# A graph layer with segment maximum: a reordered head, and a fifth matmul tile in every eighth chunk

## The chip, the core and the metric

The kernel runs on one core of one Trainium2 chip. The metric is the device time of one execution in microseconds (us). Engines are named as in the profile: PE (matmul) with its weight loads PEld, DVE (VectorE), ACT (ScalarE), POOL (GpSimd) and SP (SyncE, which here only issues DMAs). SPq, ACTq and POOLq are the queues in which DMAs are issued.

## The reference

There are 12,500 nodes with 32 features and 400,000 edges, sorted by their target node `dst`; `src` is random.

```python
h = jnp.maximum(_layernorm(x, axis=-1), 0.0)
e_feat = jnp.concatenate([h[src], h[dst], edge_attr_32], axis=-1)   # 400000 x 96
v = jax.nn.relu(e_feat @ W1 + b1) @ W2 + b2                         # 96 -> 64 -> 32
x_cand = jax.ops.segment_max(v, dst, num_segments=num_nodes)
x = x + jnp.maximum(x_cand, h)
```

## The kernel before

**Tiling.** The edges are cut into four stripes of 100,352 and these into 196 chunks of 512. A chunk is worked on for all four stripes at once, so 128 partitions hold 4 stripes x 32 features. The loop (`for c in range(0, NCH, 2)`) finishes two chunks, c and c + 1, in a step and makes ready a = c + 2 and b = c + 3. There are 98 steps.

**The three parts of the first layer** are summed in PSUM tiles `ph`, in this order: the edge features `ea` (`edges_into`, L527); the target nodes (`windows_into`, L527): the product h @ W1[32:64] is made once for all nodes and kept in DRAM as `q_d`, and since targets are sorted a chunk of one stripe needs 32 rows of it, loaded by SP as `qw` (8 loads in a step, L480), with a one-hot `of` that ACT makes from the targets `db` (`window_hots`, L486 and L487); and the source nodes `ht` (L527), which close the sum.

**Source rows.** A chunk needs 16 tiles of 128 rows of h.
- 12 are gathered by POOL, one indirect DMA each (L159), three in one buffer `gh` of 18, and transposed by DVE into `ht` (L274).
- 4 come by matmuls (`tile`, L256 to L261): the node number is split into 128 x 7 keys and 14 places. h stands in SBUF as `hs`, a sum of two rounded parts in 7 groups. For a tile, 7 x 2 matmuls 128x448 multiply one-hots `hot` with `hs` into a PSUM tile `pv`; DVE multiplies by the mask of the place (`one`, L260) and reduces over the 14 places into `gm` (L261). The one-hots are made from keys `kb` loaded from DRAM: groups 0 to 4 by DVE (L225), 5 and 6 by ACT (L234 and L235).
- The first two chunks use none of this: their rows of x are gathered ahead (`raw_gather`, 8 gathers a time into `xg`) and normalized in place (`raw_1`, `raw_2`, `raw_3`).

**Then**: ACT's relu `hid` (L574), the second layer on PE (L586), a running segment maximum as a scan of DVE over the edges (L594), with penalties `pb` that are -1e30 where a new target begins, transposes and a selection of the last edge of each target on PE (L500, L511), and writes into `top_d`, which was filled with zeros before (L547). Penalties are made in the head from `de`, the targets in another layout (L449, L450), written to DRAM (`pen_d`, L451) and loaded as `pb` for four chunks at a time, as are `ea` and `db` (`load`, L465 to L469).

**Order of work.** The order on SP, PE, DVE and ACT is that of the code, written out by hand. POOL's instructions are nearly all gathers. In a step PE does: `ph<-ht`; transposes L500; `tile(a, 1)`; `edges_into(a)`; L586; `windows_into(a)`; L511; then seven tiles without a break (a 2, a 3, b 0 to b 3, and tile 0 of the next chunk), 98 matmuls. The buffers of the head (pool `nodes`) and of the loop (pool `edges`) lie in the same memory, so the first load of the loop waits for the head's last use. Every fourteenth chunk DVE does `make_block`, seven small operations.

**The head** on SP: loads of x; `h_d` writes; `key_d`, `kb`, `de`; seven `q_d` writes; `pen_d`; then `ea`, `db`, `pb` of chunks 0 to 3 and 32 `qw` loads of chunks 0 to 3.

Of the kernel before, what the change touches and what calls it, by code (L numbers as in the profile page):

```python
# [12 lines left out]
I32 = mybir.dt.int32  # L13
# [32 lines left out]
MM = 4  # L46
MMC = range(2, NCH - 1)
SOME = 3
AHEAD = 4
# [18 lines left out]
def gnn_kernel(ctx, tc, x, src, src_mm, src_t, dst, dst_ext, lo, lo_c, ends_b, edge_attr, weights, w1, w2, b2, out):  # L68
# [21 lines left out]
    dram = ctx.enter_context(tc.tile_pool(name="dram", bufs=1, space=DRAM))  # L90
    gathered = ctx.enter_context(tc.tile_pool(name="gathered", bufs=18))

# [3 lines left out]
    top_d = [dram.tile([NP, D], F32, name=f"top_d{k}") for k in range(2)]  # L96
    key_d = dram.tile([len(MMC) * MM * P], F16, name="key_d")
    acc_d = dram.tile([NP, D], F32, name="acc_d")
# [32 lines left out]
    hs = const.tile([P, 2, A1, D, A0], F32R, name="hs")  # L131
    place_k = const.tile([P, len(MMC) * MM], F32, name="place_k")

# [19 lines left out]
    def gather(c):  # L153
        n = min(K - MM * (c in MMC), (SE - c * C) // D)
        parts = []
        for k in range(0, n, SOME):
            parts.append(gathered.tile([P, SOME, D], F32, name="gh"))
            for i in range(min(SOME, n - k)):
                nc.gpsimd.indirect_dma_start(  # L159
                    out=parts[-1][:, i, :], out_offset=None, in_=h_d[:, :],  # L160
                    in_offset=bass.IndirectOffsetOnAxis(ap=src_i[:, c, k + i:k + i + 1], axis=0))
        return parts
# [5 lines left out]
    def raw_gather(i):  # L168

        raws.append(early.tile([P, HALF, D], F32, name="xg", bufs=3))  # L170
        for k in range(HALF):
            nc.gpsimd.indirect_dma_start(
                out=raws[i][:, k, :], out_offset=None, in_=x[:, :],
                in_offset=bass.IndirectOffsetOnAxis(ap=src_i[:, i // 2, i % 2 * HALF + k:i % 2 * HALF + k + 1],
                                                    axis=0))

    for i in range(3):
        raw_gather(i)
# [4 lines left out]
    nc.vector.tensor_copy(consts, counts)  # L183
    keys = {}
    hots = {}
    masks = {}
# [11 lines left out]
    def places(start, stop):  # L198

        se = src_i[:, MMC.start + start:MMC.start + stop, K - MM:]  # L200
        pk = place_k.rearrange("p (c m) -> p c m", m=MM)[:, start:stop]
        group(pk, se)
        nc.vector.scalar_tensor_tensor(pk, pk, -float(A0), se, op0=ALU.mult, op1=ALU.add)

    def load_keys(c, queue=nc.scalar):
# [39 lines left out]
    def tile(c, m):  # L245

        if c not in MMC:
            return
        if m == 0:
            mm_rows[c] = early.tile([P, MM, D], F32, name="gm", bufs=6)  # L250
        hot = hots[c]
        e = slice(m * P, (m + 1) * P)
        po = early_ps.tile([P, C], F32, name="pv", bufs=3)[:, :D * A0]
        for k in range(A1):
            for part in range(2):
                nc.tensor.matmul(po, hot[:, k, e], hs[:, part, k].rearrange("p f a -> p (f a)"),  # L256
                                 start=(k == 0 and part == 0), stop=(k == A1 - 1 and part == 1))
        of_group = po.rearrange("p (f a) -> p f a", a=A0)
        one = early.tile([P, D, A0], F32, name="one", bufs=2)
        nc.vector.tensor_tensor(one, of_group, masks[c][:, m, None, :].to_broadcast([P, D, A0]), op=ALU.mult)  # L260
        nc.vector.tensor_reduce(mm_rows[c][:, m, :], one, axis=AX.X, op=ALU.max)  # L261

    def to_features(c, part):
# [5 lines left out]
        ht = hts[c]  # L269
        n = min(K - MM * (c in MMC), (SE - c * C) // D)  # L270
        if part < J:
            r = slice(part * SOME, min((part + 1) * SOME, n))
            if r.start < n:
                nc.vector.transpose(ht[:, r].rearrange("p k e -> p (k e)"),  # L274
                                    gh[c][part][:, :r.stop - r.start].rearrange("p k f -> p (k f)"))
        elif c in MMC:
            nc.vector.transpose(ht[:, n:].rearrange("p k e -> p (k e)"),  # L277
                                mm_rows.pop(c).rearrange("p k f -> p (k f)"))
        elif n < K:
            nc.vector.memset(ht[:, n:], 0.0)  # L280
# [26 lines left out]
    with tc.tile_pool(name="nodes", bufs=1) as pool, tc.tile_pool(name="nodes_ps", bufs=2, space=PSUM) as ps:  # L307
        sp = pool.tile([P, len(MMC) * MM], I32, name="sp")
        nc.scalar.dma_start(sp, src_mm)
        load_block(0, nc.sync)  # L310
        zero = early.tile([P, ZERO], F32, name="zero", bufs=1)
        nc.gpsimd.memset(zero, 0.0)
        h = pool.tile([P, NT, D], F32, name="h")
# [101 lines left out]
        for k in range(2):  # L415
            split_1(k)
            q_transpose(k)
        key = pool.tile([P, len(MMC) * MM], F32, name="key")
        key16 = pool.tile([P, len(MMC) * MM], F16, name="key16")
        group(key, sp, key16)  # L420
        nc.sync.dma_start(key_d.rearrange("(p e) -> p e", p=P), key16)
        load_keys(MMC.start, nc.sync)
        de = pool.tile([P, EP // P + 1], I32, name="de")
        nc.sync.dma_start(de, ap(dst_ext, 0, [[EP // P, P], [1, EP // P + 1]]))
        for i in range(len(steps)):
# [3 lines left out]
            if i < 6:  # L429
                (raw_2, raw_3, raw_1)[i % 3](i // 3 + i % 3 // 2)  # L430
            if i == 1:
                raw_gather(3)
            if i < len(pieces):
                split_2(i)
                if i + 2 < len(pieces):
                    split_1(i + 2)
        raw_2(2)
        one_hots(2, 0, BY_ACT.start)
# [8 lines left out]
        for k in range(0, EP // P, EP // P // 4):  # L447
            r = slice(k, k + EP // P // 4)
            nc.vector.tensor_tensor(pen[:, r], de[:, k + 1:k + 1 + EP // P // 4], de[:, r], op=ALU.not_equal)  # L449
            nc.scalar.activation(pen[:, r], pen[:, r], AF.Copy, scale=-LOW)  # L450
        nc.sync.dma_start(pen_d.rearrange("(p e) -> p e", p=P), pen)  # L451


    ea_v = edge_attr.rearrange("s f e -> (s f) e")
    with tc.tile_pool(name="edges", bufs=3) as pool, tc.tile_pool(name="edges_ps", bufs=1, space=PSUM) as ps:
        loaded = {}
        windows = {}
        ofs = {}
        bases = {}

        def load(c, queue=nc.scalar):
            if c % LOAD == 0:
# [5 lines left out]
                queue.dma_start(db[:, :n], ap(dst_ext, 1 + c * C, [[S, NS], [0, D], [1, n]]))  # L468
                queue.dma_start(pb[:, :n], ap(pen_d, c * C, [[S, NS], [0, D], [1, n]]))  # L469
                for k in range(c, min(c + LOAD, NCH)):  # L470
                    loaded[k] = [t[:, (k - c) * C:(k - c + 1) * C] for t in (ea, db, pb)]
            if c % 2 == 0:
                _, base = nc.values_load_multi_w_load_instructions(
# [78 lines left out]
        raw_3(3)  # L552
        for k in range(2, 4):
            gh[k] = gather(k)
            window_hots(k)
        tile(2, 0)
        to_features(2, 0)
        sm = None
        sms = []
        for c in range(0, NCH, 2):  # L560
            a, b = c + 2, c + 3
            load_keys(a + 2)
            for k in range(c + AHEAD, min(c + AHEAD + 2, NCH)):
                load(k)
# [59 lines left out]
            tile(b, 3)  # L624
            to_features(b, 3)
            to_features(b, J)
            tile(a + 2, 0)
# [168 lines left out]
```

## Time and profile before

| | us |
|---|---|
| median of 3 runs | 3001.91 (3001.52 to 3004.13) |
| the profiled execution | 2999.86 |
| its span, first to last instruction | 2998.0 |
| PE busy / weight loads busy | 2868.3 (96%) / 2312.6 (77%) |
| DVE busy | 2237.3 (75%) |
| POOL busy | 2245.8 (75%) |
| ACT busy | 1068.6 (36%) |
| gathers of h, L159: 2321, mean 946 ns | 2195.5 |
| tile matmuls, L256: 10808 of 128x448 | 2219.5 |
| mean granted clock of PE | 0.98 |

The profile is one execution, taken by the hardware profiler. A row of the timeline has the start in us from the span's start, the duration, the engine, the line, the operation, what it writes and reads, and in brackets the idle time of the engine before it with what ended that. A row of the waits has the waiting engine and line, what it waited for, the total in us, the number of times and the longest. "issue" is a wait for nothing that the profile shows. Matmuls overlap, and their ends are modelled.

### The profile page before, as it was taken

What the parts mean: (1) busy time and instruction counts of PE and PEld (TensorE: products, weight loads), DVE (VectorE), ACT (ScalarE), POOL (GpSimd) and SP (SyncE); (2) the same over time, 40 slices, a digit from 0 to 9 for tenths busy, and PEclk for the clock granted to TensorE, in tenths of its full rate; (3) what the DMA queues carried; (4) which work ended last, traced back from release to release, by engine and by line L of the source; (5) the groups of instructions that cost most, each with busy time, mean ns of one, the idle gap of its engine ahead of it and who ended that gap; (6) DMA issues with size and microseconds to landing.
All of it is one profiled execution on the core that took longest, in us unless ns stands there. A gap on an engine that the chain in (4) does not pass through costs nothing. (4 is left out here: it accounts for less than half of the span.)

```text
span 2998.0 us, 58325 instructions
## 1 busy us (share of the span) xinstructions
PE 2868.3 (96%) x21077; PEld 2312.6 (77%) x21077; DVE 2237.3 (75%) x3865; ACT 1068.6 (36%) x1693; POOL 2245.8 (75%) x2372
## 2 busy tenths in 40 slices
PE   2899999999999999999999999999999999999995
PEld 1678888788887877787777787778787878787774
DVE  5578778787787777777777777777777777777775
ACT  3333433333333333333333333333333333333331
POOL 7777777777777777777777777777777777777774
PEclk8899999999999999999999999999999999999997
DMA  6432233232233223222322232223222322232222
GB/s 201 134 76 67 70 81 75 64 81 73 71 76 79 70 60 87 70 71 60 83 70 71 59 89 69 67 63 81 73 71 59 83 75 67 63 81 74 67 54 73
DMA packets 189043, 229.40 MB, mean 77 GB/s; under 512 B 117821, under 2 KB 160461, under 8 KB 175950
## 3 DMA queue, kind: packets, MB, share of 16 engines
q10 hardware_dynamic: 26692, 110.28, 11.3%
q0 software_dynamic: 75296, 38.70, 10.3%
q1 hardware_dynamic: 86762, 76.66, 8.4%
q8 instruction: 165, 2.70, 0.4%
q14 instruction: 128, 1.05, 0.1%
HBM read 211.54 MB, written 13.85 MB: 75 GB/s over the span
## 5 line engine op out<-in xcount | busy, mean ns | idle before, releaser
L159 POOL DMA_INDIRECT gh<-h_d,src_i x2321 | 2195.5, 946 | 708.1 <-issue 529.2
L256 PE MATMUL pv<-hs,hot 128*128 128x448 f32 x10808 | 2219.5, 364 | 0.9 <-DVE sm L594 0.9
L256 PEld LDWEIGHTS pv<-hs,hot 128*128 128x128 f32 x10808 | 2016.7, 188 | 143.4 <-issue 3.2
L260 DVE TENSOR_TENSOR one<-pv,mask 128x448 f32<-128x448 f32 x772 | 477.5, 619 | 547.8 <-PE pv L256 543.9
L574 ACT ACTIVATE hid<-ph,wt 128x512 f32<-128x512 f32 x392 | 237.6, 689 | 1047.6 <-PE ph L527 825.4
L225 DVE TENSOR_TENSOR hot<-kb,consts 128x1024 fp32r<-128x1024 f16 (+2 forms) x385 | 559.2, 1452 | 0.0
L261 DVE TENSOR_REDUCE gm<-one 128x32 f32<-128x448 f32 x772 | 478.6, 620 | 26.6
L235 ACT ACTIVATE hot<-away,ones 128x512 fp32r<-128x512 f32 x386 | 279.4, 724 | 488.2 <-issue 472.5
L274 DVE STREAM_TRANSPOSE ht<-gh 128x96 f32<-128x96 f32 x774 | 208.2, 269 | 109.4 <-DMA gh<-h_d,src_i 109.4
L234 ACT ACTIVATE away<-kb,key_n 128x512 f32<-128x512 f16 x386 | 276.6, 716 | 0.0
L594 DVE TENSOR_TENSOR_SCAN sm<-pb,sm,pv 128x512 f32<-128x512 bf16 x195 | 247.5, 1269 | 11.1 <-PE pv L586 0.5
L527 PE MATMUL ph<-ht,wt 32*64 32x512 f32 x1568 | 142.1, 640 | 25.1 <-DVE ht L277 25.1
L511 PEld LDWEIGHTS pv<-so,last 128*64 128x64 f32 x3136 | 100.1, 138 | 80.4 <-PE pv L586 74.7
L500 PEld LDWEIGHTS pv<-ident,sm 128*128 128x128 f32 x784 | 89.5, 147 | 85.3 <-issue 70.8
L486 ACT ACTIVATE of<-db,below 128x512 f32<-128x512 int32 x196 | 138.8, 708 | 31.6 <-DMA db<-in_dst_ext 27.0
L487 ACT ACTIVATE of<-of,ones 128x512 f32<-128x512 f32 x196 | 142.1, 725 | 6.4
L527 PE MATMUL ph<-of,qw 32*64 32x512 f32 x1568 | 114.0, 617 | 21.0 <-DMA qw<-q_d 21.0
L515 ACT ACTIVATE wo<-pv 128x128 f32<-128x128 f32 x98 | 27.3, 278 | 298.1 <-PE pv L511 286.5
L527 PE MATMUL ph<-ea,wt 32*64 32x512 f32 x1568 | 110.1, 617 | 21.7 <-DMA qw<-q_d 21.7
L502 DVE TENSOR_TENSOR so<-pv,wt 128x512 f32<-128x512 f32 x196 | 125.2, 676 | 3.9 <-PE pv L500 3.9
L492 DVE TENSOR_TENSOR last<-consts,at 128x512 f32<-128x512 f32 x196 | 122.5, 663 | 0.0
L511 PE MATMUL pv<-so,last 128*64 128x64 f32 x3136 | 113.7, 226 | 1.4 <-DVE last L492 1.4
(80 smaller groups left out, 611.8 us busy)
## 6 DMA issues: line engine op xcount, KB each, us to landing
ea<-in_edge_attr SPq DMA_DIRECT2D x49, 1024.0 KB
db<-in_dst_ext ACTq DMA_DIRECT2D x48, 1024.0 KB
gh<-h_d,src_i POOLq DMA_INDIRECT x2321
pb<-pen_d ACTq DMA_DIRECT2D x48, 512.0 KB
kb<-key_d ACTq DMA_DIRECT2D x47, 512.0 KB
qw<-q_d SPq DMA_DIRECT2D x784, 8.0 KB
top_d<-wo SPq DMA_DIRECT2D x784, 4.0 KB
top_d<-zero ACTq DMA_DIRECT2D x2, 1568.0 KB
```

Of the source, the lines that this page charges most:

```text
L159: nc.gpsimd.indirect_dma_start(out=parts[-1][:, i, :], out_offset=None, in_=h_d[:, :], in_offset=bass.IndirectOffsetOnAxis(ap=src_i[:, c, ...
L225: nc.vector.tensor_tensor(hot_of(c)[:, start:stop], keys[c][:, None, :].to_broadcast([P, n, MM * P]), key_ps[:, start:stop, None].to_broad ...
L234: nc.scalar.activation(away, keys[c], AF.Square, bias=key_n[:, k:k + 1])
L235: nc.scalar.activation(hot_of(c)[:, k], away, AF.Relu, bias=ones, scale=-1.0)
L256: nc.tensor.matmul(po, hot[:, k, e], hs[:, part, k].rearrange("p f a -> p (f a)"), start=(k == 0 and part == 0), stop=(k == A1 - 1 and par ...
L260: nc.vector.tensor_tensor(one, of_group, masks[c][:, m, None, :].to_broadcast([P, D, A0]), op=ALU.mult)
L261: nc.vector.tensor_reduce(mm_rows[c][:, m, :], one, axis=AX.X, op=ALU.max)
L274: nc.vector.transpose(ht[:, r].rearrange("p k e -> p (k e)"), gh[c][part][:, :r.stop - r.start].rearrange("p k f -> p (k f)"))
L511: nc.tensor.matmul(pw[g * 2 * W:(g + 1) * 2 * W, x * 2 * D:(x + 1) * 2 * D], last[x][:, j, 2 * g:2 * g + 2].rearrange("p s w -> p (s w)"), ...
L527: nc.tensor.matmul(ph[s][x * HID:(x + 1) * HID], w[g], e[g], start=start, stop=stop)
L574: nc.scalar.activation(hid[s], ph[s], AF.Relu, bias=b1c)
L594: nc.vector.tensor_tensor_scan(sm, loaded.pop(c + x)[2], pv[x], before, op0=ALU.add, op1=ALU.max)
```

## The change

The number of PE's tiles rises from 4 to 5 in 24 of the 196 chunks (5, 13, ... 189), and gathers fall there from 12 to 11. The new tile has its own key load `kx` (issued by ACT at the start of a step), one-hot `hotx` for all seven groups (by DVE) and mask `maskx`, and comes after `tile(b, 3)`. There are 14 buffers `gh` instead of 18 and 4 `gm` instead of 6.

In the head, all four groups of raw gathers are issued first, each with a buffer of its own; `de` is loaded right behind the `h_d` writes; penalties are made before chunk 2's one-hots, and chunk 1's second half is normalized ahead of the loop's part. `pb` of chunks 0 to 3 is loaded behind the `qw` loads of chunks 0 and 1. Tile 0 of chunk 2 comes ahead of chunk 0's first matmuls. `make_block(0)`, the one-hots of chunks 2 and 3 and the zero writes move into the first step.

```diff
+MMX = range(5, NCH - 1, 8)
+TILES = len(MMC) * MM
...
-    gathered = ctx.enter_context(tc.tile_pool(name="gathered", bufs=18))
+    gathered = ctx.enter_context(tc.tile_pool(name="gathered", bufs=14))
...
-        n = min(K - MM * (c in MMC), (SE - c * C) // D)
+        n = min(K - MM * (c in MMC) - (c in MMX), (SE - c * C) // D)
...
-        raws.append(early.tile([P, HALF, D], F32, name="xg", bufs=3))
+        raws.append(early.tile([P, HALF, D], F32, name="xg", bufs=2 * MMC.start))
...
-    for i in range(3):
+    zero = early.tile([P, ZERO], F32, name="zero", bufs=1)
+    nc.gpsimd.memset(zero, 0.0)
+    for i in range(2 * MMC.start):
         raw_gather(i)
...
+    def load_key_x(c):
+
+        if c in MMX:
+            keys_x[c] = early.tile([P, P], F16, name="kx", bufs=1)
+            nc.scalar.dma_start(keys_x[c], ap(key_d, (TILES + MMX.index(c)) * P, [[0, P], [1, P]]))
+
+    def one_hot_x(c):
+
+        if c in MMX:
+            hots_x[c] = early.tile([P, A1, P], F32R, name="hotx", bufs=1)
+            nc.vector.tensor_tensor(hots_x[c], keys_x[c][:, None, :].to_broadcast([P, A1, P]),
+                                    key_ps[:, :, None].to_broadcast([P, A1, P]), op=ALU.is_equal)
+            masks_x[c] = early.tile([P, A0], F32, name="maskx", bufs=1)
+            i = MMX.index(c)
+            nc.vector.tensor_tensor(masks_x[c], place_ps, place_x[:, i:i + 1].to_broadcast([P, A0]),
+                                    op=ALU.is_equal)
...
-            mm_rows[c] = early.tile([P, MM, D], F32, name="gm", bufs=6)
-        hot = hots[c]
-        e = slice(m * P, (m + 1) * P)
+            mm_rows[c] = early.tile([P, MM + 1, D], F32, name="gm", bufs=4)
+        at_x = m == MM
+        hot = hots_x[c] if at_x else hots[c]
+        mask = masks_x[c] if at_x else masks[c][:, m]
+        e = slice(0, P) if at_x else slice(m * P, (m + 1) * P)
+        row = 0 if at_x else m + (c in MMX)
...
         raw_1(0)
+        de = pool.tile([P, EP // P + 1], I32, name="de")
+        nc.sync.dma_start(de, ap(dst_ext, 0, [[EP // P, P], [1, EP // P + 1]]))
...
         load_keys(MMC.start, nc.sync)
-        de = pool.tile([P, EP // P + 1], I32, name="de")
-        nc.sync.dma_start(de, ap(dst_ext, 0, [[EP // P, P], [1, EP // P + 1]]))
...
-            if i == 1:
-                raw_gather(3)
...
+        pen = pool.tile([P, EP // P], BF16, name="pen")
...
+        nc.sync.dma_start(pen_d.rearrange("(p e) -> p e", p=P), pen)
         raw_2(2)
         one_hots(2, 0, BY_ACT.start)
...
-        pen = pool.tile([P, EP // P], BF16, name="pen")
...
-        nc.sync.dma_start(pen_d.rearrange("(p e) -> p e", p=P), pen)
+        raw_1(3)
+        raw_2(3)
+        raw_3(3)
...
-                queue.dma_start(pb[:, :n], ap(pen_d, c * C, [[S, NS], [0, D], [1, n]]))
+                if c:
+                    load_pen(c, pb, queue)
...
         for c in range(AHEAD):
             load(c, nc.sync)
-        make_block(0)
+            if c == 1:
+                load_pen(0, pbs[0], nc.sync)
         for c in range(2):
             window_hots(c)
-        raw_1(3)
-        for t in top_d:
-            nc.scalar.dma_start(ap(t, 0, [[NT * D, P], [ZERO, NT * D // ZERO], [1, ZERO]]),
-                                zero[:, None, :].to_broadcast([P, NT * D // ZERO, ZERO]))
+        for k in range(2, 4):
+            gh[k] = gather(k)
+        tile(2, 0)
+        to_features(2, 0)
         ph = edges_into(0)
         windows_into(0, ph)
-        raw_2(3)
-        raw_3(3)
-        for k in range(2, 4):
-            gh[k] = gather(k)
-            window_hots(k)
-        tile(2, 0)
-        to_features(2, 0)
...
             load_keys(a + 2)
+            load_key_x(b)
...
+            if c == 0:
+                for k in (a, b):
+                    window_hots(k)
+                for t in top_d:
+                    nc.scalar.dma_start(ap(t, 0, [[NT * D, P], [ZERO, NT * D // ZERO], [1, ZERO]]),
+                                        zero[:, None, :].to_broadcast([P, NT * D // ZERO, ZERO]))
             one_hots_act(b)
...
             mask_of(a + 2)
+            one_hot_x(b)
             tile(b, 2)
...
-            if (c + 4) % BLOCK == 0 and (c + 4) // BLOCK < NB:
+            if c == 0:
+                places_x()
+            if c == 0 or (c + 4) % BLOCK == 0 and (c + 4) // BLOCK < NB:
                 make_block((c + 4) // BLOCK)
...
             tile(b, 3)
             to_features(b, 3)
+            if b in MMX:
+                tile(b, MM)
             to_features(b, J)
```

More of the change, by code (lines that the diff above doesn't have):

```diff
@@ L96, in gnn_kernel @@
     top_d = [dram.tile([NP, D], F32, name=f"top_d{k}") for k in range(2)]
-    key_d = dram.tile([len(MMC) * MM * P], F16, name="key_d")
+    key_d = dram.tile([(TILES + len(MMX)) * P], F16, name="key_d")
     acc_d = dram.tile([NP, D], F32, name="acc_d")
@@ L131, in gnn_kernel @@
     hs = const.tile([P, 2, A1, D, A0], F32R, name="hs")
-    place_k = const.tile([P, len(MMC) * MM], F32, name="place_k")
+    place_k = const.tile([P, TILES], F32, name="place_k")
+    place_x = const.tile([P, len(MMX)], F32, name="place_x")
     wt = const.tile([P, WEIGHTS], F32, name="wt")
@@ L184, in gnn_kernel @@
     keys = {}
+    keys_x, hots_x, masks_x = {}, {}, {}
     hots = {}
@@ L203, in places, with places_x @@
         nc.vector.scalar_tensor_tensor(pk, pk, -float(A0), se, op0=ALU.mult, op1=ALU.add)
+    def places_x():
+        se = src_i[:, MMX.start:MMX.stop:MMX.step, K - MM - 1]
+        group(place_x, se)
+        nc.vector.scalar_tensor_tensor(place_x, place_x, -float(A0), se, op0=ALU.mult, op1=ALU.add)
+    def load_key_x(c):
[11 more added lines that the diff above has]
+                                    op=ALU.is_equal)
     def load_keys(c, queue=nc.scalar):
@@ L259, in tile @@
         one = early.tile([P, D, A0], F32, name="one", bufs=2)
-        nc.vector.tensor_tensor(one, of_group, masks[c][:, m, None, :].to_broadcast([P, D, A0]), op=ALU.mult)
-        nc.vector.tensor_reduce(mm_rows[c][:, m, :], one, axis=AX.X, op=ALU.max)
+        nc.vector.tensor_tensor(one, of_group, mask[:, None, :].to_broadcast([P, D, A0]), op=ALU.mult)
+        nc.vector.tensor_reduce(mm_rows[c][:, row, :], one, axis=AX.X, op=ALU.max)
     def to_features(c, part):
@@ L269, in to_features @@
         ht = hts[c]
-        n = min(K - MM * (c in MMC), (SE - c * C) // D)
+        n = min(K - MM * (c in MMC) - (c in MMX), (SE - c * C) // D)
         if part < J:
@@ L277, in to_features @@
             nc.vector.transpose(ht[:, n:].rearrange("p k e -> p (k e)"),
-                                mm_rows.pop(c).rearrange("p k f -> p (k f)"))
+                                mm_rows.pop(c)[:, :K - n].rearrange("p k f -> p (k f)"))
         elif n < K:
@@ L307, in gnn_kernel @@
     with tc.tile_pool(name="nodes", bufs=1) as pool, tc.tile_pool(name="nodes_ps", bufs=2, space=PSUM) as ps:
-        sp = pool.tile([P, len(MMC) * MM], I32, name="sp")
+        sp = pool.tile([P, TILES + len(MMX)], I32, name="sp")
         nc.scalar.dma_start(sp, src_mm)
         load_block(0, nc.sync)
-        zero = early.tile([P, ZERO], F32, name="zero", bufs=1)
-        nc.gpsimd.memset(zero, 0.0)
         h = pool.tile([P, NT, D], F32, name="h")
@@ L417, in gnn_kernel @@
             q_transpose(k)
-        key = pool.tile([P, len(MMC) * MM], F32, name="key")
-        key16 = pool.tile([P, len(MMC) * MM], F16, name="key16")
+        key = pool.tile([P, TILES + len(MMX)], F32, name="key")
+        key16 = pool.tile([P, TILES + len(MMX)], F16, name="key16")
         group(key, sp, key16)
@@ L436, in gnn_kernel @@
                     split_1(i + 2)
+        pen = pool.tile([P, EP // P], BF16, name="pen")
+        for k in range(0, EP // P, EP // P // 4):
+            r = slice(k, k + EP // P // 4)
+            nc.vector.tensor_tensor(pen[:, r], de[:, k + 1:k + 1 + EP // P // 4], de[:, r], op=ALU.not_equal)
+            nc.scalar.activation(pen[:, r], pen[:, r], AF.Copy, scale=-LOW)
+        nc.sync.dma_start(pen_d.rearrange("(p e) -> p e", p=P), pen)
         raw_2(2)
@@ L443, in gnn_kernel @@
         nc.vector.tensor_tensor(below, below, lo_w, op=ALU.subtract)
-        pen = pool.tile([P, EP // P], BF16, name="pen")
[L447 to L450, printed above, removed]
-        nc.sync.dma_start(pen_d.rearrange("(p e) -> p e", p=P), pen)
+        raw_1(3)
+        raw_2(3)
+        raw_3(3)
     ea_v = edge_attr.rearrange("s f e -> (s f) e")
@@ L456, in gnn_kernel @@
         loaded = {}
+        pbs = {}
         windows = {}
@@ L459, in gnn_kernel, with load_pen @@
         bases = {}
+        def load_pen(c, pb, queue):
+            n = min(LOAD, NCH - c) * C
+            queue.dma_start(pb[:, :n], ap(pen_d, c * C, [[S, NS], [0, D], [1, n]]))
         def load(c, queue=nc.scalar):
@@ L468, in load @@
                 queue.dma_start(db[:, :n], ap(dst_ext, 1 + c * C, [[S, NS], [0, D], [1, n]]))
-                queue.dma_start(pb[:, :n], ap(pen_d, c * C, [[S, NS], [0, D], [1, n]]))
+                if c:
+                    load_pen(c, pb, queue)
                 for k in range(c, min(c + LOAD, NCH)):
                     loaded[k] = [t[:, (k - c) * C:(k - c + 1) * C] for t in (ea, db, pb)]
+                pbs[c] = pb
             if c % 2 == 0:
@@ L754 @@
     sc = np.ascontiguousarray(sp.reshape(NS, NCH, K, D).transpose(1, 2, 0, 3).reshape(NCH, K, P))
-    sm = sc[MMC.start:MMC.stop, K - MM:]
+    sm = np.concatenate([sc[MMC.start:MMC.stop, K - MM:].reshape(-1), sc[MMX.start:MMX.stop:MMX.step, K - MM - 1].reshape(-1)])
     w1, w2 = np.asarray(L0_gnn_W1), np.asarray(L0_gnn_W2)
@@ L770 @@
         "src": np.ascontiguousarray(sc.transpose(2, 0, 1).reshape(P, NCH * K)),
-        "src_mm": np.ascontiguousarray(sm.reshape(P, len(MMC) * MM)),
+        "src_mm": np.ascontiguousarray(sm.reshape(P, TILES + len(MMX))),
         "src_t": sp.reshape(NS, TS, P),
```

## The prediction

> **What bounds the kernel now.** I read four views in this order: the busy time by stretch, the waits by stretch, the timeline of one loop step, and the timeline of the head with SP's own waits. One loop step runs from one `ph<-ht` group on PE to the next, two chunks, 98 in all.
>
> By stretch (columns: stretch, its length, then busy us of PE, PEld, DVE, ACT, POOL, granted clock, DMA share, GB/s):
>
> ```profile
> 97.00:1165.00 1068.00, 1067.05 (x7942) 869.14 (x7941) 830.82 (x1438) 396.61 (x628) 807.69 (x855) 1.00 0.31 75
> 1165.00:2912.00 1747.00, 1717.14 (x12551) 1383.96 (x12553) 1308.02 (x2269) 621.89 (x986) 1320.41 (x1398) 0.99 0.29 71
> ```
>
> In the first stretch PE idles for 0.95 us of 1068, in the second for 30 of 1747. POOL's share is 76% in both. Two stages then, and the waits between 1200 and 1500 us tell what is new in the second (us in total, times, longest):
>
> ```profile
> DVE ht L274 <- DMA gh<-h_d,src_i: 20.2, 10, 3.5
> ```
>
> The answers for 300 to 600 and 600 to 900 us have no such row: gathered rows were there in time. POOL's timeline shows it in the same rhythm in both stages:
>
> ```profile
> 600.27 0.94 POOL L159 DMA_INDIRECT gh<-h_d,src_i  x1 [0.30 <-issue]
> 601.51 0.95 POOL L159 DMA_INDIRECT gh<-h_d,src_i  x1 [0.30 <-DMA gh<-h_d,src_i]
> 602.77 0.95 POOL L159 DMA_INDIRECT gh<-h_d,src_i  x1 [0.30 <-issue]
> ```
>
> One gather costs 0.95 + 0.30 = 1.251 us, always; 0.30 is its turnaround, not a wait. A step of 24 gathers is 30.02 us of POOL. PE's own step is read where it waits for nothing:
>
> ```profile
> 442.94 1.11 PE L527 MATMUL ph<-ht,wt 32*64 32x512 f32 x16
> ...
> 452.00 19.88 PE L256 MATMUL pv<-hs,hot 128*128 128x448 f32 x98
> ...
> 466.54 0.20 DVE L240 TENSOR_TENSOR mask<-consts,place_k 128x56 f32<-128x56 f32 x1
> 466.67 0.61 DVE L260 TENSOR_TENSOR one<-pv,mask 128x448 f32<-128x448 f32 x1
> ...
> 471.81 1.25 PE L527 MATMUL ph<-ht,wt 32*64 32x512 f32 x16
> ```
>
> 471.81 - 442.94 = 28.87; nearly all steps up to 1165 us are 28.88. So PE starts late (97 us), with POOL 36 gathers ahead at the second `ph<-ht` (124.13 us; 60 issued, 24 used up), catches up 0.9 gathers a step, and from 1165 us on waits for POOL. The steps from 124.13 to the last `ph<-ht` at 2957.50 last 2833.4 us. PE alone would need 95 x 28.88 + 2.9 (block and place work of DVE in 14 steps) + 16.7 (the short last step) = 2763.2. POOL is worth 70.2 us.
>
> **The fifth tile.** 24 chunks (5, 13, ... 189) get 11 gathers and one tile more.
> - POOL: -24 x 1.251 = -30.0 us.
> - PE: 98 matmuls in 19.88 us, of which the last takes its 0.36: (19.88 - 0.36)/97 = 0.201 each; 14 make 2.82 us. 24 x 2.82 = **+67.7 us**.
> - A step then averages 28.88 + 2.82/4 = 29.59 us on PE and 23.75 x 1.251 = 29.71 on POOL. POOL falls back by 0.1 gathers a step: of a lead of 36 some 26 are left at the end. POOL no longer ends last; its last gather ends at 2952 - 30 = 2922, from where the old tail (2998 - 2952 = 46) would give 2968.
> - So from the second step on the loop takes 2763.2 + 67.7 = 2830.9, against 2833.4: **-2.5 us**. One bound is exchanged for another of almost the same height.
> - DVE per extra tile: hotx, between 1.18 (1024 wide) and 0, by width 1.03; maskx under 0.20 (56 wide); `one` and reduce 0.62 each. hotx and maskx stand between the mask at 466.54 and the `one` at 466.67 and push the latter to 467.9; the next `one` can't start before its tile ends at 469.1, so 1.2 us goes into idle time. PE wants hotx at 469.1 and has it at 467.8: free, by 1.3 us. Without that cover it is 1.2 us a time, 29 in all.
> - At nothing: the kx load (32 KB; ACT, which issues it, idles 10.16 us before hid), the wider transpose and key, place_x (four small DVE operations once), gm in 4 buffers (two live). With 14 buffers of 3 gathers POOL may be 42 ahead; it is 36 to 39. If that is short, POOL's slack (2922 against 2958) pays.
>
> The Trainium skill (Perfetto Trace Analysis, Identifying the Most-Contended Engine) says that matmul busy time tells little of PE's headroom and weight-load busy time more. By it PE has 19% left in the first stretch (869 of 1068) and the tile could be almost free; that is rival D. The fixed 28.88 with 0.95 us idle speaks against it.
>
> **The head.** It is a chain; the rows that carry it:
>
> ```profile
> 57.76 0.34 SPq L465 DMA_DIRECT2D ea<-in_edge_attr  x1
> 58.15 0.70 SPq L468 DMA_DIRECT2D db<-in_dst_ext  x1
> ...
> 78.62 0.72 ACT L486 ACTIVATE of<-db,below 128x512 f32<-128x512 int32 x1 [24.52 <-DMA db<-in_dst_ext]
> ...
> 92.17 5.05 PE L256 MATMUL pv<-hs,hot 128*128 128x448 f32 x14
> ...
> 94.48 0.60 ACTq L468 DMA_DIRECT2D db<-in_dst_ext  x1
> ...
> 103.28 1.11 PE L527 MATMUL ph<-of,qw 32*64 32x512 f32 x16
> ...
> 104.32 19.88 PE L256 MATMUL pv<-hs,hot 128*128 128x448 f32 x98
> ...
> 124.13 1.11 PE L527 MATMUL ph<-ht,wt 32*64 32x512 f32 x16
> ```
>
> (1) ea and db overlie the node buffers, so they still wait for DVE's last node operation (`below`) and for pen's write. DVE order after: raw_1(2) 0.87, pen 3.62, then what took 43.92 to 49.68 before (5.76). raw_1(2) waits for gathered rows (42.56 before; 40.3 at the least, since de's 1.6 MB are now out of the way earlier); I take 42.0: 42.0 + 10.25 + 0.2 = **52.5** for ea, 5.3 us earlier. pen's write (issued 47, landing 3.0 us later by SP's wait) is no longer last.
> (2) db lands 20.9 us after ea's issue (57.76 to 78.62): 73.3. Four `of` activations (78.62 to 81.46): 76.1. The first tile lies before that now, and the first `ph<-ht` comes near 78, against 97.16. Were this all, the gain would be some 19 us.
> (3) It isn't. SP's waits in 50 to 130 us:
>
> ```profile
> SPq L480 <- DMA db<-in_dst_ext: 30.2, 2, 15.2
> SPq L480 <- DMA pb<-pen_d: 7.6, 2, 4.9
> SPq L480 <- DMA top_d<-zero: 1.8, 2, 1.6
> ```
>
> qw loads have nothing to do with db, pb or zero: they wait because SP's and ACT's DMAs share eight semaphores in turn, and a DMA waits until the earlier one on its semaphore has landed. In the built order of the new kernel the third qw load of chunk 2 shares with **db of chunks 4 to 7**, and the last of chunk 3 with **pb of chunks 4 to 7**. ACT issues those two right after `of`, at 76.2. All eight loads are needed by `windows_into(2)` in step 0, so PE stands from about 88 until pb(4) has landed. Before, these two waited for the two zero writes instead.
> (4) When is that? SP's queue, which carries db, is busy for a quarter of 16 engines (0.20 to 0.27 between 65 and 77.5 us): four engines, in order. pb(0), now issued after db(0), at 74.3, moves from 75.8; the four then do pb(0) 5.4 (78.4 to SP's next issue at 83.76), db(4) 16 (first packet to last takes 13.8 to 17.7 in thirty loads), pb(4) 5.4: 102.6. Bounds: two queues on one engine may overlap, -5; pb's packets spread over up to 10.9 us, +5. qw after that 2.5, its matmuls 0.5: the burst of 98 starts at **105.6**, against 104.32.
> (5) PE has idled and runs at half clock: 92.17 to 97.16 shows 14 matmuls in 5.05 instead of 3.06 after such a pause: +2.1 (bounds 0 and 4). Second `ph<-ht`: 124.13 + 1.3 + 2.1 = **127.5**.
>
> The Trainium skill (DMA: Bandwidth & Descriptors, How many engines (k)) has a transfer use the largest number up to 16 that divides its slowest dimension: four here, as the trace shows. Its figure of 27 GiB/s for one engine would pass (4)'s 512 KB in 18 us and make the total 9 us less; db's own 256 KB in 16 us say slower.
>
> The eight raw gathers that move ahead of gh's cost POOL nothing in sum; memset zero (0.44) goes ahead of them. The zero writes now queue behind pb(4) on ACT's ring, and the second holds ACT until a qw load behind db(4) lands, near 100; what ACT has next (chunk 3's one-hots, 2.9 us) is wanted at 113.
>
> **Sum.** +3.4 - 2.5 = +0.9 us on the profiled execution (2999.86, 1.86 above its span of 2998.0): 3000.8. The median of the runs lies 2 above it (3001.91): **3002.8**. The head's gain is eaten by a wait that takes the old one's place, and the loop exchanges POOL for PE.
>
> **Rivals.**
> - B, the window loads don't hold PE: `windows_into(2)` runs near 84. The second `ph<-ht` comes near 107: 3002 - 17 - 2.5 = 2982. For it: ea is earlier anyhow, and a shared semaphore shows only in the built order. Against: such waits do show in SP's rows (30.2 us).
> - C, slower: in the 24 steps PE finds hotx not ready. Place: DVE between the next chunk's mask and the `one` after it. Price up to 1.2 us each, 29: 3032; it decides once DVE is 1.3 us later than in the step above. Block work (2.1 us) coincides in four of the steps.
> - D, the tile fits into PE's slack (the change costs nothing on PE): POOL's end decides, 2968 + 1.9 + 2 = 2972. For it: weight loads busy 81%. Against: 28.88, always.
> - That loads don't wait for penalties is only half true: ea still does, by (1). It is in the forecast.
>
> **How the numbers follow.** A measurement here can tell about 0.2%, 6 us. Forecast A: 0.62, 2995 to 3009 by the bounds in (1), (4), (5); within it 0.05 faster than -6 and 0.07 slower than +6. B 0.14, C 0.18 (0.02 of it too small to be told), D 0.06. Faster 0.25, same 0.52, slower 0.23. The range takes in A, B and C up to some 0.6 us a step: 2981 to 3016; D and the rest of C, 0.15, stay out.
>
> **What would show it.** Steps of 28.88 and 31.7 up to the end; no waits of DVE for gh; POOL's last gather near 2922. ea issued at 52 to 53. A pause of PE between about 88 and 105, with SP's qw waiting for db and pb. Second `ph<-ht` at 124 to 131. Wrong if that pause is absent (B), if the long steps exceed 32 (C) or stay at 29 (D).

## The result, and the profile after

The changed kernel takes 3043.09 us (median of 4 runs, 3039.27 to 3044.33), the kernel before on the same chip 3003.02 (4 runs, 3001.52 to 3004.73): a ratio of 1.0127, 95% interval 1.0115 to 1.0140. It is **slower by 40 us**; 3002.8 was forecast, and the range ended at 3016. The profiled execution took 3039.27 us, its span 3037.5, against 2998.0.

Cut at the two `ph<-ht` groups that the prediction used, the 39.5 us of span lie in one place:

| | before | after | difference |
|---|---|---|---|
| start to second `ph<-ht` | 124.1 | 126.2 | +2.1 |
| second to last `ph<-ht` | 2833.4 | 2869.9 | **+36.5** |
| last `ph<-ht` to the end | 40.5 | 41.4 | +0.9 |

The head is as forecast. PE's timeline (start, length, then operation) shows the pause, and behind it the burst of 98. The first seven gaps from start to start of its matmuls are 358 to 540 ns, the others 201 to 207; the granted clock is 0.50 from 98 to 104 us and 0.56 in the four after that.

```profile
83.14 1.09 PE L624 MATMUL pv<-hid,wt 64*32 64x512 f32 x16
85.45 1.04 PE L564 MATMUL ph<-of,qw 32*64 32x512 f32 x2 [1.22 <-DMA qw<-q_d]
98.87 2.86 PE L564 MATMUL ph<-of,qw 32*64 32x512 f32 x12 [12.38 <-DMA qw<-q_d]
102.87 1.96 PE L564 MATMUL ph<-of,qw 32*64 32x512 f32 x2 [1.14 <-DMA qw<-q_d]
104.77 21.52 PE L288 MATMUL pv<-hs,hot 128*128 128x448 f32 x98
126.21 1.83 PE L564 MATMUL ph<-ht,wt 32*64 32x512 f32 x16
```

SP's own waits between 50 and 130 us (us, times, longest) name the cause that step (3) named:

```profile
SPq L517 <- DMA db<-in_dst_ext: 30.8, 2, 17.0
SPq L517 <- DMA pb<-pen_d: 2.5, 1, 2.5
```

The 17.0 us are the third `qw` load of chunk 2, which waits for db of chunks 4 to 7, and the 2.5 us the last one of chunk 3, which waits for their pb, both as forecast. The other 13.8 us are a `qw` load of chunk 1 behind the first db; it costs nothing, since `of` waits for that db too. The trace also shows the eight semaphores that the DMAs of SP and ACT take in turn.

In the loop, the table by stretch (stretch, its length, then busy us of PE, PEld, DVE, ACT, POOL, granted clock, DMA share, GB/s) shows a PE that never stands, at a granted clock of 1.00:

```profile
126.20:1165.00 1038.80, 1038.80 (x7625) 837.63 (x7625) 803.17 (x1390) 371.72 (x591) 777.44 (x822) 1.00 0.29 70
```

DVE's waits between 127 and 2990 us have no row for gathered rows at all. So POOL is off the path, as intended, and PE is the bound. But PE does the same work more slowly. A long step and two ordinary ones behind it, from PE's timeline:

```profile
367.45 1.11 PE L564 MATMUL ph<-ht,wt 32*64 32x512 f32 x16
...
376.54 17.43 PE L288 MATMUL pv<-hs,hot 128*128 128x448 f32 x84
393.81 3.00 PE L288 MATMUL pv<-hs,hotx 128*128 128x448 f32 x14
396.65 3.01 PE L288 MATMUL pv<-hs,hot 128*128 128x448 f32 x14
399.59 1.11 PE L564 MATMUL ph<-ht,wt 32*64 32x512 f32 x16
...
408.70 20.19 PE L288 MATMUL pv<-hs,hot 128*128 128x448 f32 x98
428.82 1.11 PE L564 MATMUL ph<-ht,wt 32*64 32x512 f32 x16
...
437.92 20.30 PE L288 MATMUL pv<-hs,hot 128*128 128x448 f32 x98
458.15 1.11 PE L564 MATMUL ph<-ht,wt 32*64 32x512 f32 x16
```

From one `ph<-ht` to the next it is 29.23 and 29.33 us in turn where it was 28.88, and nearly the whole difference stands in the burst of 98 tile matmuls: 20.19 and 20.30 us in place of 19.88. (The other tile of the step, 14 matmuls, takes 0.02 to 0.04 us more.) The groups that aren't tile matmuls have kept their lengths. Taken from start to start of its matmuls and averaged over the burst (**the pitch**), it went from 201.2 ns a matmul to 204.4 in one step and 205.5 in the next, all the way to the end. Long steps take 32.14 us, and each stands in the place of a step of 29.33: the tile with `hotx` costs 2.81 us, where 2.82 were reckoned. Over the loop the steps are 0.39 us longer on average, and 95 of them are 37 us: the loss.

What could slow the same instructions by 2%? Nothing in the diff touches them. But the diff changes the sizes of what lies ahead of them in SBUF, the memory that the engines work in: `gathered` lost four buffers of 384 bytes in each partition, `xg` gained one of 1024, and `place_x` came in with 96. That makes 416 bytes less. `hs`, the moving operand (the one that streams through PE), lies ahead of all three and stayed at byte 46304 of each partition; `hot`, the stationary operand (the one that is loaded as weights), went from 109472 to 109056.

### The profile page after: what moved, and what is told of

It reads as the page before. It is cut to its first block, busy times and chain, and to the rows that moved or that the text cites. A ratio compares the mean times of both kernels' runs of the same rounds, so it can differ in the third digit from the quotient of the medians.

```text
span 3037.5 us, 59139 instructions
## 1 busy us (share of the span) xinstructions
PE 2939.1 (97%) x21413; PEld 2363.5 (78%) x21413; DVE 2294.2 (76%) x3965; ACT 1067.9 (35%) x1693; POOL 2225.5 (73%) x2348
## 5 line engine op out<-in xcount | busy, mean ns | idle before, releaser
L288 PE MATMUL pv<-hs,hot 128*128 128x448 f32 x10808 | 2259.6, 368 | 8.2 <-DVE hot L254 8.2
L293 DVE TENSOR_REDUCE gm<-one 128x32 f32<-128x448 f32 x796 | 493.8, 620 | 27.4
L632 DVE TENSOR_TENSOR_SCAN sm<-pb,sm,pv 128x512 f32<-128x512 bf16 x195 | 247.5, 1269 | 10.7 <-PE pv L624 0.5
L306 DVE STREAM_TRANSPOSE ht<-gh 128x96 f32<-128x96 f32 (+1 forms) x774 | 206.9, 267 | 3.4 <-DMA gh<-h_d,src_i 3.4
L564 PE MATMUL ph<-ht,wt 32*64 32x512 f32 x1568 | 113.5, 617 | 1.8 <-DVE ht L309 1.8
L564 PEld LDWEIGHTS ph<-of,qw 32*64 32x64 f32 x1568 | 24.2, 131 | 115.2 <-issue 95.8
```

Of the source, the lines that this page charges most:

```text
L293: nc.vector.tensor_reduce(mm_rows[c][:, row, :], one, axis=AX.X, op=ALU.max)
L564: nc.tensor.matmul(ph[s][x * HID:(x + 1) * HID], w[g], e[g], start=start, stop=stop)
L632: nc.vector.tensor_tensor_scan(sm, loaded.pop(c + x)[2], pv[x], before, op0=ALU.add, op1=ALU.max)
```

## The experiments

**Theory P**: the place of `hot` sets the pitch. **Rival Q**: it is what runs beside the matmuls, now that POOL, DVE and the DMAs are busy to the end, with fewer gather buffers. **Rival C** of the prediction, `hotx` late on PE, is out already by the stretch above (PE idles 0.00 us in it), though long steps do exceed 32.

### Four places of `hot`

In three kernels made of the changed one, `gm` has 3 buffers instead of 4 to make room, and an unused tile is put ahead of `hot`, or behind it:

```
+            if not hots:
+                early.tile([P, 8], F32, name="pad", bufs=1)
             hots[c] = early.tile([P, A1, MM * P], F32R, name="hot", bufs=2)
```

32 bytes ahead:

> The changed kernel with 32 bytes put ahead of the one-hots `hot` (gm has 3 buffers instead of 4 to make room), so that `hot` starts at 109088 instead of 109056, a remainder of 32 instead of 0 by 64, as in the kernel before (109472); `hotx` goes the other way (remainder 0). Theory P64 (the place of the stationary operand, by its remainder of 64, sets the matmul pitch): the pitch inside the bursts of 98 goes back from 204 to 206 ns to 201, steps from 29.23 to 28.88 us, hotx's pitch up to 204 or more, time about 3043 - 37 = 3006. Theory P512 (only the old remainder, 416 by 512, or the old address is quick): 204 to 206 as after, 3043. Theory Q (not the place: what the new kernel does beside the matmuls, POOL, DVE and DMA busy to the end): 204 to 206, 3043.

416 bytes ahead:

> The changed kernel with 416 bytes ahead of `hot` (gm has 3 buffers): both buffers of `hot` stand at the very addresses of the kernel before, 109472 and 123808. P64 and P512: pitch 201 ns, steps 28.88 us, time about 3006. Q: 204 to 206 ns, 29.23 us, 3043.

32 bytes behind, the control:

> Control: gm in 3 buffers and the 32 bytes behind `hot` instead of ahead of it, so that `hot` stays where the changed kernel has it (109056) and all that follows it lies as in the run with the 32 bytes ahead. P64 and P512: pitch 204 to 206 ns, 29.23 us, 3043. If the places of the tiles behind it (gm, one, the edge buffers) or gm's buffers matter instead: 201 ns and about 3006. Q: 3043.

And 32 bytes ahead in the kernel before:

> The kernel before with 32 bytes ahead of `hot`: 109504, a remainder of 0 by 64. P64: pitch 204 to 206 ns and PE-bound steps of 29.2 to 29.3 us in the first 1100 us; the time stays within 6 us of 3003, since POOL (30.02 us a step, its last gather near 2952) ends last in either case. P512 (every place but the old one is slow): the same. Q: pitch 201, steps 28.88.

One burst of each, from PE's timeline: 32 ahead, 416 ahead, 32 behind, then the kernel before with 32 ahead.

```profile
467.03 20.09 PE L290 MATMUL pv<-hs,hot 128*128 128x448 f32 x98
```

```profile
465.59 19.88 PE L290 MATMUL pv<-hs,hot 128*128 128x448 f32 x98
```

```profile
442.12 20.19 PE L290 MATMUL pv<-hs,hot 128*128 128x448 f32 x98
```

```profile
460.50 20.51 PE L258 MATMUL pv<-hs,hot 128*128 128x448 f32 x98
```

| kernel | `hot` at | pitch, ns | ordinary step, us | time, us (before 2997.66) |
|---|---|---|---|---|
| changed, 416 ahead | 109472 | 201.2 | 28.88 | 3004.73, ratio 1.0023 (1.0013 to 1.0032) |
| changed, 32 ahead | 109088 | 203.3 | 29.11 | 3024.69, 1.0090 (1.0073 to 1.0107) |
| changed, 32 behind | 109056 | 204.4 | 29.23 | 3040.54, 1.0141 (1.0124 to 1.0158) |
| before, 32 ahead | 109504 | 207.6 | 29.57 | 3002.26, 1.0017 (1.0008 to 1.0027) |

`hot` back in its old place gives the old pitch, with all of the change still in: Q falls. The control moves what lies behind `hot` by the same 32 bytes, has the same three buffers `gm`, and stays slow: for those 32 bytes it is `hot`, not its neighbours. Both forms of P that were put first fall too: 32 bytes bring back a third of the pitch, where the remainder by 64 promised all of it and the old address alone (P512) nothing. The time follows the pitch, from 3004.73 to 3040.54.

In the kernel before, the slowest pitch of all (207.6 ns, where 204 to 206 were expected) costs only 4.6 us. Its waits show why (DVE, 130 to 2940 us; the kernel before, then the one with 32 bytes):

```profile
DVE ht L274 <- DMA gh<-h_d,src_i: 109.4, 60, 4.4
```

```profile
DVE ht L276 <- DMA gh<-h_d,src_i: 6.1, 7, 1.9
```

There POOL was the bound, and PE's longer steps only filled the time in which DVE had waited for gathered rows. The change took that cover away. That is why the loss shows in full in the new kernel, and hardly at all in the old one.

### The burst by itself, at 128 places

A kernel that leaves out the whole computation and only runs the loop's bursts of 98, with nothing beside PE, at places 32 bytes apart:

```
+    for dh, dw in PLACES:
+        for k in range(8):
+            nc.tensor.matmul(sep[:D], mid[:HID, :D], mid[:HID, 512:1024], start=True, stop=True)
+        for buf, m in ((0, 2), (0, 3), (1, 0), (1, 1), (1, 2), (1, 3), (0, 0)):
...
+            for k in range(A1):
+                for part in range(2):
+                    w = (dw + buf * BUF) // 4 + k * MM * P + m * P
+                    h = dh // 4 + (part * A1 + k) * D * A0
+                    nc.tensor.matmul(p[:, :D * A0], hot[:, w:w + P], hs[:, h:h + D * A0],
+                                     start=(k == 0 and part == 0), stop=(k == A1 - 1 and part == 1))
```

> The disputed cost by itself. The kernel leaves out the whole computation (its output is zeros): PE alone runs bursts of 98 matmuls in the form of the loop's (two buffers 14336 bytes apart, the same order of slices), with hs at its real address 46304 and the first buffer at 109056 + 32 j, j from 0 to 127, then with hs moved by 32 and more bytes. Nothing else runs beside it. If the pitch is PE's own matter and follows the addresses of its two operands (theory P), the bursts repeat the whole kernels: near 201 ns at 109472, 203 to 204 at 109088, 204 to 206 at 109056, 207 to 208 at 109504. If it is hot's address against hs's that counts, moving both by 32 bytes changes nothing (201 for hs + 32 and hot 109504). If the address only matters through other engines' reads and writes in the same memory (theory N), all bursts have one pitch.

Eight bursts in order, `hot` at 109184 and then 32 bytes on each time, from PE's timeline:

```profile
128.00 20.39 PE L110 MATMUL pv<-hs,hot 128*128 128x448 f32 x98
...
155.30 19.88 PE L110 MATMUL pv<-hs,hot 128*128 128x448 f32 x98
...
182.09 19.87 PE L110 MATMUL pv<-hs,hot 128*128 128x448 f32 x98
...
208.87 20.12 PE L110 MATMUL pv<-hs,hot 128*128 128x448 f32 x98
...
235.91 20.19 PE L110 MATMUL pv<-hs,hot 128*128 128x448 f32 x98
...
263.01 20.09 PE L110 MATMUL pv<-hs,hot 128*128 128x448 f32 x98
...
290.01 20.51 PE L110 MATMUL pv<-hs,hot 128*128 128x448 f32 x98
...
317.43 20.25 PE L110 MATMUL pv<-hs,hot 128*128 128x448 f32 x98
```

With PE alone at work the pitch still differs by place, so theory N falls. The pattern repeats after eight places, 256 bytes, sixteen times over (but for the first burst of the run, which begins with thirteen gaps of 373 to 539 ns). By the distance from `hs` to `hot`, as a remainder of 256:

| distance | 0 | 32 | 64 | 96 | 128 | 160 | 192 | 224 |
|---|---|---|---|---|---|---|---|---|
| pitch, ns | 203.8 | 204.4 | 203.3 | 207.7 | 205.1 | 206.4 | **201.2** | 201.1 |

With `hs` moved by 32 bytes the row of numbers moves by one place: it is the distance that counts, not the place of `hot` alone. The kernel before has 63168, a remainder of 192; the changed one 62752, a remainder of 32; 32 bytes ahead make it 64. All three agree with the whole kernels to 0.1 ns, apart from the 205.5 of every other step, which the bursts at distance 32 also show in their repetitions.

That the table isn't all, 224 shows: 201.1 here, but 207.6 in the kernel before with 32 bytes ahead, where one burst of 96 ran at 201.2. In the repetitions of this kernel it came out as 207.6 once and 201.1 five times. Distances 0 and 96 also gave 207.7 and 201.2, in the last bursts, where `hs` moved and `hot` stood. So the pitch is a rhythm that the stream of weight loads and matmuls falls into, and at some distances there are two of them; what decides between them was not shown. In the kernel before the gaps run 201, 197, 202 ns, over and over; in the changed one 201, 206, 207 in the slower rhythm. Distance 192 gave 201.2 each time here.

The Trainium skill (TensorE: Matmul & The Clock Gate, Step-by-step: what each phase is for) says that PE reads the two operands through two independent ports, and that loading the next weights takes no read bandwidth from the running matmul. Read by itself, that leaves no room for the distance to matter; the 201.1 to 207.7 ns above, from PE alone, show that it does.

One more look, whether the distance decides in the whole kernel too. The kernel before, with 32 bytes ahead of `hs`, so that both move:

```
+    const.tile([P, 8], F32, name="pad")
     hs = const.tile([P, 2, A1, D, A0], F32R, name="hs")
```

> The kernel before with 32 bytes ahead of hs, so that hs (46336) and hot (109504) both move by 32 and their distance stays what it was (63168, a remainder of 192 by 256), while hot stands where the run with 32 bytes ahead of hot had it. If the distance of the two operands sets the pitch, as the bursts alone say: 201 ns and steps of 28.88 us. If the address of hot itself counts: 207 to 208 ns and 29.57 us, as in that run.

```profile
451.97 19.88 PE L257 MATMUL pv<-hs,hot 128*128 128x448 f32 x98
```

All 96 bursts ran at 201.1 to 201.2 ns, with steps of 28.88 us, and the one run took 2996.67 us (before 2998.07). `hot` stands at 109504 as in the run with 207.6 ns: its own address isn't what counts.

### Where the head's gain went

The prediction said that 19 us of the head are eaten by qw loads that wait for db and pb of chunks 4 to 7. On top of the 416 bytes, these two go on SP's queue, behind the qw loads:

```
-                load(k)
+                load(k, nc.scalar if c else nc.sync)
```

> The changed kernel with hot at 109472 (as in the run with 416 bytes ahead) and, besides, db and pb of chunks 4 to 7 on SP's queue instead of ACT's, so that the qw loads of chunks 2 and 3 no longer share semaphores with them. By the prediction's step (3) the pause of PE between 86.5 and 98.9 us goes, and half speed after it: the second ph<-ht comes near 110 instead of 128.6, and the time is some 15 to 18 us below the run with 416 bytes alone: near 2988. If the pause has another cause (db, of, one-hots or POOL late), the second ph<-ht stays at 124 or later and the time at 3000 to 3005.

Measured 2996.28 us, ratio 0.9996 (0.9986 to 1.0005): 8 us better than with the 416 bytes alone, not 17. The pause is gone, and the second `ph<-ht` comes at 104.2 instead of 128.6. But 15 us are lost one step later. PE's timeline, then ACT's wait behind it (104 to 121 us):

```profile
104.16 2.01 PE L566 MATMUL ph<-ht,wt 32*64 32x512 f32 x16
...
106.94 3.06 PE L290 MATMUL pv<-hs,hot 128*128 128x448 f32 x14
119.72 3.71 PE L566 MATMUL ph<-ea,wt 32*64 32x512 f32 x16 [9.72 <-ACT hid L608]
```

```profile
ACT hid L608 <- DMA qw<-q_d: 14.1, 1, 14.1
```

hid needs no qw. ACT stands at its kb load, which shares a semaphore with a qw load of chunks 6 and 7; SP issues that one late, since it waits 24.3 us for the zero writes of `top_d` in the same way. It is the same mechanism one link on. So the zero writes were moved up as well, behind the penalties:

```
+        for t in top_d:
+            nc.scalar.dma_start(ap(t, 0, [[NT * D, P], [ZERO, NT * D // ZERO], [1, ZERO]]),
+                                zero[:, None, :].to_broadcast([P, NT * D // ZERO, ZERO]))
...
             if c == 0:
                 for k in (a, b):
                     window_hots(k)
-                for t in top_d:
-                    nc.scalar.dma_start(ap(t, 0, [[NT * D, P], [ZERO, NT * D // ZERO], [1, ZERO]]),
-                                        zero[:, None, :].to_broadcast([P, NT * D // ZERO, ZERO]))
```

> The run with hot at 109472 and db, pb of chunks 4 to 7 on SP, and besides the two zero writes of top_d issued by ACT right after the penalties (about 46 us) instead of in the loop's first step (82 us), where they held semaphores that kb's load, and ACT behind it, waited for (14.1 us ahead of hid). If that wait is what took the gain of the run before back: no pause of PE between 108 and 120, third ph<-ht some 31 us behind the second instead of 46.7, and the time 10 to 17 us lower, 2979 to 2987; db lands up to 8 us later, because the zero writes now move beside it. If it wasn't: 2994 to 3000.

This forecast missed: 2996.72 us, 0.9999 (0.9989 to 1.0008), no gain in the median. Step two does shrink, from 46.7 to 34.3 us, but ea is issued at 54.4 instead of 50.7 (SP waits 7.4 us for pen's write, which moves beside the zero writes at a DMA share of 0.90 to 1.03), and `of` starts 24.4 us after that (78.76): the second `ph<-ht` falls back to 111.5. Its profiled span is 5.1 us shorter, 2988.9 against 2994.0; the median doesn't bear that out.

With the zero writes out of the loop, db itself is last: its last packet ends at 78.0 us, and `of` starts at 78.76. It is cut into its four stripes:

```
+                    for s in range(NS):
+                        queue.dma_start(db[s * D:(s + 1) * D, :n], ap(dst_ext, 1 + s * S, [[0, D], [1, n]]))
```

> As the run with the zero writes moved, and the first db load as four transfers, one for each stripe, of 32 rows each, instead of one that lies on four DMA engines (it landed 20 us after ea's issue, at a DMA share of 0.24 to 0.32). If db's four engines bound the head: db lands 8 to 13 us sooner, and the time is that much lower, 2970 to 2977; POOL, which gathers without a pause from 49 to 2919 us, bounds it below near 2968. If ea, pb or the zero writes bound it: no change, 2979 to 2987. Against the kernel before, 3 to 28 us faster.

By stretch from 61 to 66 us, when the zero writes are over, first the run before, then this one (DMA share and GB/s at the end of the line):

```profile
61.00:66.00 5.00, 2.02 (x16) 0.36 (x16) 0.00 (x0) 0.00 (x0) 3.78 (x5) 0.50 0.47 117
```

```profile
61.00:66.00 5.00, 0.56 (x8) 0.36 (x16) 0.00 (x0) 0.00 (x0) 3.78 (x4) 0.50 1.05 217
```

From 62 to 66 us four of db's packets are under way at a time in the run before, and 15 in this one. The issue of ea and the start of `of`, in the same order:

```profile
54.40 0.34 SPq L505 DMA_DIRECT2D ea<-in_edge_attr  x1
...
78.76 0.72 ACT L528 ACTIVATE of<-db,below 128x512 f32<-128x512 int32 x1 [21.86 <-DMA qw<-q_d]
```

```profile
54.59 0.34 SPq L505 DMA_DIRECT2D ea<-in_edge_attr  x1
...
70.43 0.72 ACT L532 ACTIVATE of<-db,below 128x512 f32<-128x512 int32 x1 [13.35 <-DMA qw<-q_d]
```

`of` starts 15.8 us after ea's issue instead of 24.4, and the time is 2987.39 us, **0.9966 (0.9954 to 0.9979) of the kernel before**: the one version here that beats both kernels, the one before by 10.7 us. That is 9.3 us below the run before, about as much as `of` starts sooner (8.3). The forecast's 2970 to 2977 was missed because it counted down from 2979 to 2987, which the run before had not reached. The second step is still 38.6 us long (31.7 without a wait): hid waits 7.7 us for the same shared semaphores. By the Trainium skill (DMA: Bandwidth & Descriptors, How many engines (k)) a slowest dimension of 32 rows goes to 16 engines where four stripes went to four; the 15 packets against four agree with it.

Last, whether the repaired head is worth anything without the fifth tile. The same kernel with one such chunk instead of 24 (`hot` kept in place):

```
-MMX = range(5, NCH - 1, 8)
+MMX = range(5, 6, 8)
```

> The run with db split, but the fifth tile in one chunk instead of 24 (23 gathers more; hot kept at 109472). By the prediction's loop accounting POOL ends last again: 2320 gathers of 1.251 us from 49.7 us end near 2952, and with the 46 us behind the last gather of the kernel before the span is 2998: near 2999, as the kernel before, and the repaired head alone is worth nothing; DVE waits for gh in the second half, and steps average 30.0 us there. If the head's 20 us count without the tile, the time stays at 2987 or falls with PE's 65 us less, down to 2922.

**Inconclusive.** It was run three times, and each time on a chip on which the kernel before itself took 4292 to 4303 us; the ratios there were 0.9981 (0.9944 to 1.0018), 0.9956 (0.9920 to 0.9991) and 0.9979 (0.9933 to 1.0026). The granted clock was 0.88 to 0.90 there, against 0.98, and PE's instructions themselves come late:

```profile
PEld ph L573 <- issue: 573.2, 581, 10.7
```

Steps last 42 us, and POOL's longest waits are for DVE to free its buffers. What the fifth tile is worth beside the repaired head stays open. An estimate from rows of the run with db split: 23 more gathers of 1.251 us would move its last one from 2919.6 to some 2948 us, and with the 46 us that follow the last gather in the kernel before the span is 2994, some 10 us above the 2984.4 of that run. No run here shows it.

## Why the prediction was wrong, step by step

- **The failed step** is the one that carried the loop over: "A step then averages 28.88 + 2.82/4 = 29.59 us on PE". The 28.88, and the 0.201 of a tile matmul in it, were taken from the profile of before, for instructions that the diff doesn't touch, and were held to be a property of the instruction. They are a property of it and of where its two operands lie, and the change moved one of them by 416 bytes. Measured: 29.23 and 29.33 in turn. The same loop with `hot` in the old place takes 2832.9 us from the second to the last `ph<-ht`, in the new place 2869.9: 36.9 us, the whole error of the loop but 2.
- **The tile's own price held**: 2.82 forecast, 2.81 measured (32.14 against the 29.33 whose place it takes), and 2.80 with `hot` in its old place (31.68 against 28.88). It was the 98 matmuls already there that grew dearer.
- The prediction did look at the 14 buffers, for what they do to POOL's lead. That four buffers less, with the new `xg` and `place_x`, also move everything behind them wasn't seen.
- **The loop's exchange was right.** 2830.9 forecast, 2832.9 measured with the placement undone; no wait for gathered rows. POOL's last gather began at 2954.69, where the forecast had it end at 2922, because PE's slower steps held the buffers; in the run with 416 bytes it began at 2925.02.
- **The head was right** in its mechanism and nearly to the number: ea issued at 52.08 (52.5 forecast), `of` at 71.56 (73.3), the pause from 86.5 to 98.9 (88 to 105.6 with the loads behind it), the burst at 104.77 (105.6), the second `ph<-ht` at 126.2 (127.5). That the last numbers agree so well is in part luck: pb of chunks 4 to 7 landed at 98.4, 4 us sooner than reckoned (102.6), and the last `qw` and its matmuls then took 6.4 us instead of 3.0. The runs above confirm the cause: with these waits gone the pause is gone.
- With the placement undone the change as a whole is 7.1 us slower than before (1.0023), against 0.9 forecast. Of the 5.9 us between the two profiled spans 4.5 lie in the head, 1.9 behind the last `ph<-ht` and -0.4 in the loop. So what the forecast reckoned with was there, within its range; what it left out, 36.9 us, was some forty times its sum of 0.9.
- **Rivals.** B is out: qw did hold PE. C is out: between 127 and 2990 us PE has no wait for `hotx`. Its mark, long steps above 32 us, came true for another reason; a mark that two causes can make does not tell them apart, and the difference between a long step and the one whose place it takes (2.81) does. D is out: the tile costs its full price.

## What to carry to other kernels

When a diff changes the size or number of any buffer, compare the addresses of the operands of the hottest matmuls before and after, and read the pitch of one burst in each profile before looking for waits. Where PE is the bound, the placement of its two operands is a knob (up to 3.3% of a burst here), and an unused tile of a few hundred bytes sets it; where another engine is the bound, it is hidden and comes out when that bound goes. DMAs on two queues that share semaphores in turn pass a long transfer's wait on to loads that have nothing to do with it: follow it link by link, since the first one removed only shows the next.

## What the runs showed of the hardware

- The pitch of a stream of 128x128 loads and 128x448 matmuls of fp32r depends on the distance of the two operands in SBUF, with a period of 256 bytes over the 4096 bytes tried in steps of 32: 201.1 to 207.7 ns, 3.3%, with PE alone at work. Steps of 4 bytes matter too, in one burst each: from distance 192 on, 204.4, 201.1, 204.5, 205.4 and 209.9 ns for 4, 8, 12, 16 and 20 bytes more. Why 256, and what sets which of two rhythms a burst falls into, wasn't found.
- The recorded lengths hardly show it: the median weight load is 188 ns before and after, the median matmul 363 and 366 ns. The distance from start to start does.
- With 1 MB of targets as one transfer, four of its packets at a time, `of` could start 24.4 us after the load ahead of it was issued; cut into four transfers of 32 rows, with 15 packets at a time, 15.8 us after it.
- The DMAs of SP and ACT take eight semaphores in turn in these kernels, and a DMA is issued only when the earlier one on its semaphore has landed: a `qw` load waited 17.0 us for a load of targets that it has nothing to do with.
